# Maxima over all slots by VectorE's block transposes in place of TensorE's, in four of five groups

## The chip, the cores and the metric

The kernel runs on one core of a Trainium2 chip. A core has a matrix engine (TensorE, PE in the profile; its weight loads are listed apart as PEld), three engines for elementwise work (VectorE or DVE, ScalarE or ACT, GpSimd or POOL), a queue for transfers (SyncE or SP) and 16 DMA engines. Each engine works through its own queue in order, and engines wait for each other through semaphores. Matrix products are written to PSUM; the other operands lie in SBUF, on 128 partitions. The metric is the device time of one execution in microseconds, as a median over runs.

## The reference

Sixteen sequences of 100 tokens, 256 wide, go through cross attention to a context of 361 tokens (16 heads), and then through a soft mixture of 16 experts with 64 slots each. Everything is float32. What matters here is the second half, cut to its core:

```python
x = _layernorm(x, norm_g, norm_b)
se = _layernorm(slot_embeds, slot_g, slot_b) * scale
logits = jnp.einsum('bnd,esd->bnes', x, se)
dispatch = jax.nn.softmax(logits, axis=1)
combine = jax.nn.softmax(logits.reshape(x.shape[0], x.shape[1], -1), axis=-1)
slots = jnp.einsum('bnd,bnes->besd', x, dispatch)
gate = jax.nn.gelu(jnp.einsum('besd,edf->besf', slots, Wg) + bg, approximate=False)
up = jnp.einsum('besd,edf->besf', slots, Wu) + bu
eout = jnp.einsum('besf,efo->beso', gate * up, Wd) + bd
return jnp.einsum('bns,bso->bno', combine, eout)
```

`combine` is a softmax over all 1024 slots of a token. It needs, for each token, the largest logit over the slots. That maximum is what the change concerns.

## The kernel before

The 16 sequences are cut into groups of 2, 2, 4, 4 and 4 (`GROUPS`, line 51). A group goes through attention (`units`, line 862: for each sequence and each of four blocks of heads the scores, their maxima, the exponentials and the values), then through `dispatch_quarter` for each pair p of sequences and each quarter q of the 1024 slots, then through `combine_weights` for each pair, and at last through `experts` with `combine_quarter`. The experts of one group run beside the attention of the next.

The program is fixed when it is built. A planner in the kernel (`Clock`, line 64, and the loop from line 1361) keeps a modelled time for each engine; every piece of work is a generator that yields when it would be ready, how many PSUM banks it needs and, in some cases, the word "aside". At each step the planner issues the first piece in a list that is ready at the modelled time of PE (units and dispatches, then side work, then the experts). From the first expert on, a step marked "aside" is held until VectorE's modelled backlog is at most 2.5 us (`BACKLOG`, lines 1417 to 1421). Four PSUM banks, tiles tagged "mm", go round among all products except the attention scores. Of several `combine_weights` in the list only the first is looked at, so that pairs follow one another.

In `dispatch_quarter` (line 927) the logits of a pair lie with 128 slots on the partitions and (two slot blocks, two sequences, 100 tokens) along the row. They are copied to `lg_all` (line 963), and `top` (128 partitions by 2 by 100) takes the maximum over the blocks seen so far (lines 1064, 1065, 1068). After four quarters `top` holds on each partition the maximum over eight of the 1024 slots, and the maximum over the 128 partitions is still to come.

`combine_weights` (line 1073) does this with TensorE. Two transposes (line 1079) turn `top` into `top_t`, 100 tokens by 256, in PSUM; VectorE reduces each row (line 1081) to the negative maximum `c_mx`; VectorE multiplies the identity by it (line 1089), giving two diagonal matrices `dg`; a product of ones with `dg` (line 1093) puts the negative maximum of each token on all 128 partitions of `neg_top`; ScalarE copies it back into `top` (line 1100). A float32 product is two instructions in the profile, a transpose is one. Then GpSimd adds it to the logits of each quarter (line 1107), ScalarE takes the exponentials (line 1130), GpSimd sums them into `dg` (lines 1133, 1134, 1137), and a product with ones gives the sums over the slots (line 1119, `c_sums`), whose reciprocal `combine_quarter` uses. There are eight pairs in all, one in each of the first two groups and two in each of the others.

Three other places serve for comparison. `dispatch_quarter` transposes by VectorE within blocks of 32 from group 3 on (line 1012, `BY_DVE`). `key_work` does so for the context of sequences 4 and up (lines 598, 599). In attention, VectorE's reduction of line 790 (`mxp`) and the addition of line 801 (`q`) stand between products of PE (lines 785, 799, 810).

Of the kernel before, what the change touches and what calls it, by code (L numbers as in the profile page):

```python
# [33 lines left out]
F32 = mybir.dt.float32  # L34
AF = mybir.ActivationFunctionType
ALU = mybir.AluOpType
AX = mybir.AxisListType
# [3 lines left out]
B, N, D = 16, 100, 256  # L41
# [6 lines left out]
P = 128  # L48
# [81 lines left out]
def xattn_ffn_kernel(  # L130
# [27 lines left out]
    nc = tc.nc  # L158
    ctx.enter_context(tc.manual_schedule())
    ck = Clock(4)  # L160

    const = ctx.enter_context(tc.tile_pool(name="const", bufs=1))
    dram = ctx.enter_context(tc.tile_pool(name="dram", bufs=1, space=DRAM))
    two = ctx.enter_context(tc.tile_pool(name="two", bufs=2))
# [4 lines left out]
    def mm_tile(name):  # L169
        return ps_mm.tile([P, 512], F32, tag="mm", name=name)  # L170
# [52 lines left out]
    ident = const.tile([P, P], F32, name="ident")  # L223
# [105 lines left out]
    ones = const.tile([P, P], F32, name="ones")  # L329
# [439 lines left out]
    class Unit:  # L769
# [35 lines left out]
        def exponentials(self):  # L805

            for c in range(3):
                for r in range(4):
                    rows = slice(32 * r, 32 * r + 32)
                    nc.tensor.matmul(  # L810
                        self.at[: KC + 1, r, c * N : (c + 1) * N],
                        lhsT=self.k[rows, c * KC : c * KC + KC + 1],
                        rhs=self.q2[rows],
                        start=True,
                        stop=True,
                    )
            self.aT = two.tile([P, 4, 3 * N], F32, tag="aT", name="aT")
            nc.scalar.activation(self.aT[: KC + 1], self.at[: KC + 1, :, : 3 * N], AF.Exp)  # L818
            self.t = free_t[0] = ck.act("exp", 1080, ck.run("PE", 0.85, self.t))
            phase[0] = "exp"  # L820
            if self.cb == 3:
                live.discard(self.b)
# [104 lines left out]
    def dispatch_quarter(g, p, q):  # L927
# [142 lines left out]
        top[1] += 1  # L1070
        logits[g, p, q] = slot

    def combine_weights(g, p):

        yield (lambda: tops[g, p][2] if tops.get((g, p), (0, 0))[1] == NQ else NEVER), 1
        top, _, t = tops[g, p]
        tp = mm_tile("top_t")
        for i in range(2):
            nc.tensor.transpose(tp[:N, i * P : (i + 1) * P], top[:, i, :], ident)
        nm = two.tile([N, 2], F32, tag="c_mx", name="c_mx")  # L1080
        nc.vector.tensor_reduce(
            nm, tp[:N, : 2 * P].rearrange("n (i s) -> n i s", i=2), AX.X, ALU.max, negate=True
        )
        t = ck.psum_dve(256, ck.run("PE", 0.25, t, ck.bank()))
        ck.free(t)

        dg = const.tile([P, 2, N], F32, tag="dg", name="dg")
        for i in range(2):
            nc.vector.tensor_scalar_mul(dg[:N, i, :], ident[:N, :N], nm[:, i : i + 1])
            t = ck.run("DVE", 0.22)  # L1090
        yield t, 1
        ps = mm_tile("neg_top")
        nc.tensor.matmul(
            ps[:, : 2 * N],
            lhsT=ones[:N, :],
            rhs=dg[:N].rearrange("n i t -> n (i t)"),
            start=True,
            stop=True,
        )
        nc.scalar.copy(top.rearrange("p i n -> p (i n)"), ps[:, : 2 * N])  # L1100
        t = ck.copy(200, ck.pe(200, t, ck.bank()))
        ck.free(t)
        tq = [t]
        for q in range(NQ):
            yield tq[-1], 0
            w = lg_all[:, logits[g, p, q]].rearrange("p (c i) n -> p c i n", c=2)
            nc.gpsimd.tensor_tensor(w, w, top.unsqueeze(1).to_broadcast([P, 2, 2, N]), ALU.add)
            t = ck.run("POOL", 0.9, t)
            tq.append(t)
            if q:  # L1110
                yield tq[-2], 0
                tq[-2] = exponentials(g, p, q - 1, dg, tq[-2])
        yield tq[-1], 0
        t = exponentials(g, p, NQ - 1, dg, tq[-1])
        yield t, 1
        sm = const.tile([N, 2], F32, tag=f"c_sm{p}", name="c_sm", bufs=2)
        ps = mm_tile("c_sums")
        for i in range(2):
            nc.tensor.matmul(
                ps[:N, i : i + 1], lhsT=dg[:, i, :], rhs=ones[:, 0:1], start=True, stop=True  # L1120
            )
        nc.vector.reciprocal(sm, ps[:N, :2])
        t = ck.run("DVE", 0.2, ck.run("PE", 0.5, t, ck.bank()))
        ck.free(t)
        sums[g, p] = sm
# [235 lines left out]
    while streams["experts"]:  # L1361
        g = len(accs)
# [110 lines left out]
        if task.done:  # L1473
            fill[:] = [t for t in fill if t is not task]
            dispatches[:] = [t for t in dispatches if t is not task]
            for name, t in streams.items():
                if t is task:
                    streams[name] = None
                    if name == "units":
                        g = group - 1  # L1480
                        for p in range(GROUPS[g] // 2):
                            for q in range(NQ):
                                dispatches.append(Task(dispatch_quarter(g, p, q), ck, 2))
                            dispatches.append(Task(combine_weights(g, p), ck))
# [52 lines left out]
```

## Time and profile before

| what | value |
|---|---|
| median of 3 runs | 1176.27 us (1175.8 to 1177.32) |
| the profiled execution | 1176.62 us, its span 1174.70 us |
| granted TensorE clock, mean | 0.999 |
| DVE, ACT, POOL busy | 632.8 us, 542.9 us, 153.6 us |
| PEld busy | 899.3 us |
| first and last transpose of `top` (line 1079) | at 113.0 us and 1050.2 us |
| last `c_sums` (line 1119) | at 1072.2 us |

The span runs from the first to the last instruction; the 1.9 us by which the execution is longer lie outside it. In groups of instructions, `out<-in` are the program's names for tiles, and L1079 is line 1079 of the kernel. Busy time of PE is the union of its instructions' spans; since they overlap, the cost of one is better read from the distance between starts. In lists of waits the columns are the time in all, the number of waits and the longest. In listings of one line or tile, three durations in ns are the least, the median and the largest.

### The profile page before, as it was taken

Reading aid. Unit: us, or ns where it says so; the run is one execution under the profiler, and the core shown is the slowest. Engines: PE = TensorE matmul, PEld = TensorE weight load, DVE = VectorE, ACT = ScalarE, POOL = GpSimd, SP = SyncE. Lnnn points to the kernel's source line nnn. Section 1 sums busy time; section 2 is a strip of 40 time slices with the busy share of each in tenths; the row PEclk is TensorE's granted clock in tenths of the full one; section 3 lists DMA queues with packets and bytes.
Section 4 is the critical chain, followed back from the end, with each engine's and each line's share of the span. In section 5 each row is a group of like instructions: output and inputs, shape, how many; then the busy total and the mean of one; then the engine's idle time right before and its main releaser. Section 6 shows DMA issues by size and latency. Waiting matters only on the chain.

```text
span 1174.7 us, 24302 instructions
## 1 busy us (share of the span) xinstructions
PE 1159.4 (99%) x9825; PEld 899.3 (77%) x9825; DVE 632.8 (54%) x1561; ACT 542.9 (46%) x1112; POOL 153.6 (13%) x255
## 2 busy tenths in 40 slices
PE   8899999999999999999999999999999999999998
PEld 6587778778788777777777777787878878777876
DVE  5755545575644667644756655657533455432222
ACT  3557554655454765554435545446312336314110
POOL 3110301022000141400101000034000003002000
PEclk9999999999999999999999999999999999999999
DMA  4412656543467404232323213333344343345441
GB/s 134 137 38 99 233 174 203 163 148 114 139 213 233 115 20 86 78 113 95 83 80 108 95 38 113 113 126 112 113 155 145 113 149 127 112 132 161 138 131 55
DMA packets 138588, 144.85 MB, mean 123 GB/s; under 512 B 45050, under 2 KB 97228, under 8 KB 138476
## 3 DMA queue, kind: packets, MB, share of 16 engines
q1 hardware_dynamic: 137258, 141.50, 39.1%
q8 instruction: 78, 1.28, 0.5%
q0 software_dynamic: 496, 1.12, 0.3%
q10 hardware_dynamic: 722, 0.67, 0.2%
q14 instruction: 34, 0.28, 0.1%
HBM read 141.60 MB, written 1.66 MB: 122 GB/s over the span
## 4 chain that ended last, share of the span: by engine, by line
PE 97%; DVE 2%; ACT 1%; POOL 0%; issue 0%; DVEq 0%; POOLq 0%; ACTq 0%
PE gp L1291 20%; PE dn L1244 19%; PE up L1291 19%; PE sl L1032 5%; PE po L1162 5%; PE at L810 5%; PE at L785 4%; PE v_ps L673 4%; PE lg L942 4%; PE k_ps L613 3%; PE cx L833 3%; PE at L1344 1%; PE o_ps L726 1%; PE q_ps L538 1%; DVE mxp L790 1%; PE d_t L1020 1%
## 5 line engine op out<-in xcount | busy, mean ns | idle before, releaser
L1291 PE MATMUL gp<-ring,w_all 128*128 128x256 f32 (+1 forms) x1280 | 249.7, 341 | 1.8 <-ACT lg_all L963 1.3
L1291 PE MATMUL up<-ring,w_all 128*128 128x256 f32 (+1 forms) x1280 | 247.2, 339 | 0.0
L1307 DVE SCALAR_TENSOR_TENSOR hT<-up,parT,ge 128x256 f32<-128x256 f32 (+1 forms) x320 | 119.4, 423 | 224.6 <-PE up L1291 179.5
L1302 ACT ACTIVATE ge<-gp,parT 128x256 f32<-128x256 f32 (+1 forms) x320 | 116.9, 429 | 266.2 <-PE gp L1291 265.6
L1244 PE MATMUL dn<-w_all,hT 128*64 128x256 f32 x2048 | 232.5, 382 | 0.0
L1291 PEld LDWEIGHTS gp<-ring,w_all 128*128 128x128 f32 x1280 | 203.7, 191 | 30.1 <-issue 8.0
L1291 PEld LDWEIGHTS up<-ring,w_all 128*128 128x128 f32 x1280 | 205.0, 191 | 21.2 <-issue 0.8
L1244 PEld LDWEIGHTS dn<-w_all,hT 128*64 128x64 f32 x2048 | 142.4, 137 | 78.1 <-issue 8.9
L1253 DVE TENSOR_TENSOR ring<-dn,bd_bc 128x512 f32<-128x512 f32 x64 | 44.3, 692 | 144.0 <-PE dn L1244 143.9
L790 DVE TENSOR_REDUCE mxp<-at 100x4 f32<-100x1444 f32 x64 | 106.3, 1660 | 28.6 <-PE at L785 26.9
L818 ACT ACTIVATE aT<-at 121x1200 f32<-121x1200 f32 x64 | 74.9, 1170 | 49.3 <-PE at L810 45.0
L1302 ACT ACT_TABLE_LOAD x61 | 78.3, 1283 | 26.4 <-PE gp L1291 25.6
L1012 DVE STREAM_TRANSPOSE disp<-d_ex 32x128 f32<-32x128 f32 x256 | 77.3, 302 | 4.6
L717 POOL TENSOR_TENSOR cxs<-cxs,rs 128x100 f32<-128x100 f32 x63 | 24.9, 397 | 385.3 <-DVE rs L714 343.3
L1032 PE MATMUL sl<-disp,xn 100*128 100x256 f32 x256 | 63.0, 388 | 0.0
L997 POOL TENSOR_TENSOR d_ex<-d_ex,d_sm 128x400 f32<-128x400 f32 x28 | 23.7, 852 | 293.5 <-DVE d_sm L994 293.4
L1162 PE MATMUL po<-ring,lg_all 128*100 128x256 f32 x256 | 59.7, 382 | 0.1
L1047 ACT ACTIVATE ring<-sl,parT 128x256 f32<-128x256 f32 x64 | 32.6, 561 | 53.1 <-PE sl L1032 53.1
L810 PEld LDWEIGHTS at<-q,kT 32*121 32x121 f32 x1344 | 40.6, 180 | 19.8 <-issue 6.1
L818 ACT ACT_TABLE_LOAD x35 | 44.9, 1283 | 22.8 <-DVE q L801 12.5
L1032 PEld LDWEIGHTS sl<-disp,xn 100*128 100x128 f32 x256 | 46.6, 190 | 9.6 <-issue 2.8
L810 PE MATMUL at<-q,kT 32*121 32x100 f32 x1344 | 49.9, 277 | 3.6 <-DVE q L801 3.6
(152 smaller groups left out, 1273.0 us busy)
## 6 DMA issues: line engine op xcount, KB each, us to landing
w_all<-in_L_ffn_Wg_dram SPq DMA_DIRECT2D x80, 512.0 KB
w_all<-in_L_ffn_Wu_dram SPq DMA_DIRECT2D x80, 512.0 KB
w_all<-in_L_ffn_Wd_dram SPq DMA_DIRECT2D x80, 512.0 KB
bd_bc<-in_L_ffn_bd_dram SPq DMA_DIRECT2D x80, 64.0 KB
c_sb<-in_ctx_dram SPq DMA_DIRECT2D x96, 44.0 KB
acc<-in_x_dram SPq DMA_DIRECT2D x7, 200.0 KB
out_dram<-acc SPq DMA_DIRECT2D x7, 200.0 KB
ring<-n_L_ffn_slot_embeds_dram POOLq DMA_DIRECT2D x1, 1024.0 KB, 7.2
```

What stands on the lines that cost most here:

```text
L673: nc.tensor.matmul(ps[: KC + 1, :D], lhsT=cT[:, kd, c * KC : c * KC + KC + 1], rhs=w_sb["wv"][:, kd, :], start=kd == 0, stop=kd == KD - 1,)
L785: nc.tensor.matmul(self.at[:N, r, :S2], lhsT=self.q[rows], rhs=self.k[rows], start=True, stop=True)
L790: nc.vector.tensor_reduce(mxv[:, :, m : m + 1], self.at[:N, :, :S2], AX.X, ALU.max, negate=True)
L810: nc.tensor.matmul(self.at[: KC + 1, r, c * N : (c + 1) * N], lhsT=self.k[rows, c * KC : c * KC + KC + 1], rhs=self.q2[rows], start=True, ...
L818: nc.scalar.activation(self.aT[: KC + 1], self.at[: KC + 1, :, : 3 * N], AF.Exp)
L1012: nc.vector.transpose(dst[toks, :, :, a, :], src[32 * a : 32 * a + 32, :, :, toks])
L1032: nc.tensor.matmul(sl[:, kd * 256 : (kd + 1) * 256], lhsT=xns[g][:, b0 + i, kd * P : (kd + 1) * P], rhs=disp[:, i, :], start=True, stop=True,)
L1162: nc.tensor.matmul(pos[i][:N, :D], lhsT=lg_all[:, slot, 2 * c + i, :], rhs=eouts_of(g, q)[:, c, 2 * p + i, :], start=c == 0, stop=c == 1,)
L1244: nc.tensor.matmul(dn[S * x : S * x + S, i * D : (i + 1) * D], lhsT=hts[x][fc // FB][0].rearrange("p (f b s) -> p f b s", f=FB, s=S)[:, fc ...
L1291: nc.tensor.matmul(ps[:, f * T : (f + 1) * T], lhsT=w[:, kd, fc * P : (fc + 1) * P], rhs=slots_of(g, q)[:, j, kd].rearrange("p b s -> p (b ...
L1302: nc.scalar.activation(ge[:, cols], ps[:, cols], AF.Gelu, bias=col(8, e, fc))
L1307: nc.vector.scalar_tensor_tensor(out=hT[:, cols], in0=ps[:, cols], scalar=col(NPAR, e, fc), in1=ge[:, cols], op0=ALU.add, op1=ALU.mult,)
```

## The change

In groups 1 to 4 (seven of the eight pairs) the maximum over the 128 partitions is found by VectorE alone. The partitions are folded by two maxima, 128 to 64 and 64 to 32. The 32 rows that are left, padded from 100 to 128 tokens, are transposed within blocks of 32, so that the 32 partial maxima of a token lie in a row; they are reduced to the negative maximum, spread over 32 columns by a copy, and four more transposes of blocks, one for each quarter of the partitions, put the negative maximum of each token on all 128 partitions. GpSimd then adds from `m2` and not from `top`. Two tiles of 128 by 256 are set to zero by GpSimd once, at the first such pair. Group 0 keeps the old way. The steps are marked "aside"; their prices in the planner are 0.7, 1.0 and four times 0.35 us of VectorE.

```diff
+    maxs = []
+    MAX_DVE = 1
...
-        tp = mm_tile("top_t")
-        for i in range(2):
-            nc.tensor.transpose(tp[:N, i * P : (i + 1) * P], top[:, i, :], ident)
-        nm = two.tile([N, 2], F32, tag="c_mx", name="c_mx")
-        nc.vector.tensor_reduce(
-            nm, tp[:N, : 2 * P].rearrange("n (i s) -> n i s", i=2), AX.X, ALU.max, negate=True
-        )
-        t = ck.psum_dve(256, ck.run("PE", 0.25, t, ck.bank()))
-        ck.free(t)
-
         dg = const.tile([P, 2, N], F32, tag="dg", name="dg")
...
+        if g >= MAX_DVE and not maxs:
+            for i in range(2):
+                maxs.append(const.tile([P, 2, P], F32, name=f"maxs{i}"))
+                nc.gpsimd.memset(maxs[i], 0.0)
+        if g >= MAX_DVE:
+
+            m2, m1 = maxs[0], maxs[1]
+            yield t, 0, (0.0, 0.7, 0.0), "aside"
+            nc.vector.tensor_tensor(m2[:64, :, :N], top[:64], top[64:], ALU.max)
+            nc.vector.tensor_tensor(m1[:32, :, :N], m2[:32, :, :N], m2[32:64, :, :N], ALU.max)
+            t = ck.run("DVE", 0.7, t)
+            yield t, 0, (0.0, 1.0, 0.0), "aside"
+            flat1, flat2 = (m.rearrange("p i n -> p (i n)") for m in (m1, m2))
+            nc.vector.transpose(flat2[:32], flat1[:32])
+            nm = two.tile([32, 8], F32, tag="c_mx32", name="c_mx32")
+            nc.vector.tensor_reduce(
+                nm, flat2[:32].rearrange("p (j s) -> p j s", s=32), AX.X, ALU.max, negate=True
+            )
+            nc.vector.tensor_copy(
+                flat1[:32].rearrange("p (j s) -> p j s", s=32),
+                nm.unsqueeze(2).to_broadcast([32, 8, 32]),
+            )
+            t = ck.run("DVE", 1.0, t)
+
+            for a in range(4):
+                if a % 2 == 0:
+                    yield t, 0, (0.0, 0.7, 0.0), "aside"
+                nc.vector.transpose(flat2[32 * a : 32 * a + 32], flat1[:32])
+                t = ck.run("DVE", 0.35, t)
+            minus = m2[:, :, :N]
+        else:
...
+            minus = top
...
-            nc.gpsimd.tensor_tensor(w, w, top.unsqueeze(1).to_broadcast([P, 2, 2, N]), ALU.add)
+            nc.gpsimd.tensor_tensor(w, w, minus.unsqueeze(1).to_broadcast([P, 2, 2, N]), ALU.add)
```

Under `else` stand the old lines: the two transposes, the reduction, the two diagonal matrices, the product with ones and ScalarE's copy.

More of the change, by code (lines that the diff above doesn't have):

```diff
@@ L1088, in combine_weights @@
[L1088 to L1101, printed above, removed]
@@ L1102, in combine_weights @@
-        ck.free(t)
+        dg = const.tile([P, 2, N], F32, tag="dg", name="dg")
+        if g >= MAX_DVE and not maxs:
[27 more added lines that the diff above has]
+        else:
+            tp = mm_tile("top_t")
+            for i in range(2):
+                nc.tensor.transpose(tp[:N, i * P : (i + 1) * P], top[:, i, :], ident)
+            nm = two.tile([N, 2], F32, tag="c_mx", name="c_mx")
+            nc.vector.tensor_reduce(
+                nm, tp[:N, : 2 * P].rearrange("n (i s) -> n i s", i=2), AX.X, ALU.max, negate=True
+            )
+            t = ck.psum_dve(256, ck.run("PE", 0.25, t, ck.bank()))
+            ck.free(t)
+            for i in range(2):
+                nc.vector.tensor_scalar_mul(dg[:N, i, :], ident[:N, :N], nm[:, i : i + 1])
+                t = ck.run("DVE", 0.22)
+            yield t, 1
+            ps = mm_tile("neg_top")
+            nc.tensor.matmul(
+                ps[:, : 2 * N],
+                lhsT=ones[:N, :],
+                rhs=dg[:N].rearrange("n i t -> n (i t)"),
+                start=True,
+                stop=True,
+            )
+            nc.scalar.copy(top.rearrange("p i n -> p (i n)"), ps[:, : 2 * N])
+            t = ck.copy(200, ck.pe(200, t, ck.bank()))
+            ck.free(t)
+            minus = top
```

## The prediction

> **What bounds the kernel now.** I read the page first: busy time, then the chain of work that ended last.
>
> ```profile
> span 1174.7 us, 24302 instructions
> PE 1159.4 (99%) x9825; PEld 899.3 (77%) x9825; DVE 632.8 (54%) x1561; ACT 542.9 (46%) x1112; POOL 153.6 (13%) x255
> PE 97%; DVE 2%; ACT 1%; POOL 0%; issue 0%; DVEq 0%; POOLq 0%; ACTq 0%
> ```
>
> PE carries 97% of the chain, VectorE 2%. A busy PE is not yet a PE at its pace, so I then read what PE itself waited for, over the whole span (total us, times, longest).
>
> ```profile
> PE at L810 <- DVE q L801: 3.6, 9, 0.8
> ...
> PE gp L1291 <- ACT lg_all L963: 1.3, 1, 1.3
> PE c_sums L1119 <- POOL dg L1134: 1.0, 1, 1.0
> ...
> PE d_t L1020 <- ACT cxs L842: 0.5, 1, 0.5
> PE gp L1291 <- DVE hT L1307: 0.5, 1, 0.5
> ```
>
> The same list by stretches puts 3.0 of the 3.6 us at line 810 into the first 60 us, and only 2.2 us of waits of all kinds behind 250 us (1.0, 0.5, 0.2 and 0.5). The code is altered from the second pair on, whose transposes start at 251.9 us, so everything ahead of that should stay as it is. The table of busy time by stage (span of the stage, then PE, PEld, DVE, ACT, POOL) shows how much room the helpers have where the seven pairs lie.
>
> ```profile
> 240.00:415.00 175.00, 174.19 (x1885) 137.91 (x1884) 102.71 (x248) 100.57 (x202) 24.24 (x39) 1.00 0.52 161
> 415.00:500.00 85.00, 84.02 (x838) 63.08 (x839) 59.19 (x140) 48.32 (x110) 29.68 (x41) 1.00 0.25 64
> 758.00:830.00 72.00, 71.52 (x434) 56.44 (x434) 45.35 (x127) 33.79 (x68) 22.22 (x34) 1.00 0.38 126
> 975.00:1075.00 100.00, 100.00 (x594) 79.59 (x592) 44.61 (x119) 42.57 (x81) 18.93 (x25) 1.00 0.43 136
> ```
>
> PE is full in each; VectorE is at 59%, 70%, 63% and 45%. So the time is that of PE's queue, and an edit is worth what it takes out of that queue, less any hole that it opens.
>
> **What leaves PE.** Durations overlap, so I take distances between starts, from the order of time around the second pair (start us, us):
>
> ```profile
> 251.25 0.72 PE L833 MATMUL cx<-aT,vpad 120*32 120x100 f32 x24
> 251.91 0.42 PE L1079 MATMUL top_t<-ident,top 128*100 128x128 f32 x2
> 252.17 1.95 PE L1291 MATMUL up<-ring,w_all 128*128 128x128 f32 x16
> 253.95 0.25 PE L799 MATMUL at<-ident,mxp 100*128 100x100 f32 x1
> 254.09 0.58 PE L1093 MATMUL neg_top<-dg,ones 100*128 100x200 f32 x2
> 254.50 0.39 PE L1291 MATMUL gp<-ring,w_all 128*128 128x128 f32 x2
> ```
>
> The two transposes hold PE from 251.91 to 252.17, 0.26 us; the product with ones from 254.09 to 254.50, 0.41 us. The same reading for the seven pairs gives 0.26, 0.31, 0.26, 0.31, 0.22, 0.26 and 0.36 us for the transposes (1.98 in all) and 0.41, 0.43, 0.43, 0.54, 0.34, 0.34 and 0.44 us for the product (2.94): 4.92 us. From below, the steps inside these groups are 109 ns for a transpose and 169 ns for a half of the product, so 7 x (2 x 0.109 + 2 x 0.169) = 3.9 us is pure streaming, and the other 1.0 us is change-over between shapes, of which some may return at the new neighbours. From above, a down product that is followed by something else steps by 310 ns and not by 216, so 7 x 0.094 = 0.7 us more may go with the interruptions: 5.6 us. I take 4.9, the distances that were really there.
>
> **What leaves the others.** ScalarE loses seven copies of 0.33 us (2.3 us) and VectorE seven reductions of 0.42 and fourteen multiplications that take 0.45 us a pair: 0.87 us a pair. PSUM's four banks lose two uses a pair. None of it is on PE's path today: nothing in PE's list waits for `top_t`, `c_mx` or `neg_top`. I count 0.
>
> **What VectorE gains.** The trace has no operation on these very shapes, so I price by the nearest rows (least/median/largest ns):
>
> ```profile
> L1064 DVE TENSOR_TENSOR top<-top,lg_all x24: 347/356/368, 95.4 to 1046.6; 128x200 f32<-128x200 f32 x24
> L967 DVE TENSOR_REDUCE d_mx<-lg_all x28: 569/570/571, 210.4 to 1012.2; 128x4 f32<-128x400 f32 x28
> L1012 DVE STREAM_TRANSPOSE disp<-d_ex x256: 289/302/308, 565.8 to 1042.6; 32x128 f32<-32x128 f32 x128
> L598 DVE STREAM_TRANSPOSE cT<-c_sb x12: 855/910/915, 192.5 to 669.8; 128x704 f32<-128x704 f32 x12
> L418 DVE COPY ring<-pat x1: 400/400/400, 15.0 to 15.0; 128x256 f32<-128x256 f32 x1
> ```
>
> Two maxima over 200 elements: 2 x 0.36. Five transposes over 256: between 302 ns for 128 and 910 for 704 a straight line gives 0.44, so 2.2. One reduction of 256 elements: 0.42, as the one that goes. One copy with a repeated input: 0.40. Together 3.7 us a pair, net 2.9, over seven pairs 20 us on an engine that was busy for 633 of 1175. The bounds are wide: with 0.25 (line 801, 100 elements) for maxima, copy and each transpose (line 599, 64 elements) the work is 2.4 us a pair; with 0.91 for each transpose, 0.57 for the reduction and 0.69 for the copy (line 1253, 512 elements) it is 6.5. I take 3.7, since the rows on either side of 256 elements are close. The planner prices it at 3.1, so VectorE runs behind its plan by 0.6 us a pair (-0.7 to +3.4 by the bounds).
>
> What hides this is the plan: the work is in four pieces of about 0.8 to 1.3 us, each held while VectorE's backlog is over 2.5 us, and PE has products that do not need VectorE. Queued behind a piece are the attention's reduction (line 790) and addition (line 801), PSUM evacuations (lines 1307, 1253, 1044) and `d_mx`; behind those stand PE's lines 799 and 810 and the four banks. Without cover a pair costs PE up to 2.9 us, 20 us in all. Behind 250 us PE waited for VectorE 0.2 us at line 810 and 0.5 us at line 1291, so I cost it at 0, with 0 to 4.4 us (the lag of 0.6, seven times) as what may show.
>
> **New waits.** The first maximum waits for GpSimd's two zero fills: by the row of 128x112 in 0.19 us, about 0.44 each, 0.1 to 1.0. GpSimd is idle from 251.0 to 255.3, so they are done before VectorE comes to them; at worst 0.9 us of VectorE, once. Writing `m2` again waits for the adds of line 1107 of the pair ahead; the fourth add ends 12 to 17 us after its pair begins, and the pairs begin at least 43 us apart. The adds now wait for the last transpose in place of ScalarE's copy, which itself sat in ScalarE's queue (423.3 us for a product that ended at 420.6). So the sums come from some us earlier to some later; only `c_sums` and, far behind, `combine_quarter` wait for them, and the experts pass over a quarter whose sums are missing. `c_sums` already cost PE 0.98 us once, at 439.2 us, where a GpSimd addition took 2.08 us in place of 0.61.
>
> The Trainium skill, page SBUF — State Buffer, section "SBUF: two separate sides", says that VectorE and GpSimd lock a pair of SBUF ports against each other for whole instructions, where VectorE reads two SBUF inputs or uses both ports. By it the two maxima and the copy, 1.1 us a pair, could each hold GpSimd up, 7.8 us in all, and if all of that reached `c_sums` the time would be 1179.5 us. The trace has long additions (2.08 and 1.78 us), but VectorE was then mostly in line 790's reduction from PSUM, and a pair's own additions start after its maxima; I leave the sum as it is.
>
> **Sum.** 1176.6 - 4.9 + 0 = 1171.7 us, against the profiled execution's own time (span 1174.7, and 1.9 outside). That execution is 0.35 us above the median of the runs.
>
> **Rivals.**
> *The gain is given back (1174 to 1178, about 1176).* A new order of all that follows 250 us opens new holes. The lag of 0.6 us a pair, if it all shows, is 4.4 us: 1176.1. For it: `c_sums` and line 810 do wait at times. Against it: 2.2 us of holes in 925 us says that the plan fills nearly everything.
> The Trainium skill, page Perfetto Trace Analysis, section "Identifying the Most-Contended Engine", warns that matmul occupancy is no measure, and points to weight-load time, here 77%; by that PE would have room and the removal might bring nothing, 1176.6. The starts speak against it: 16 instructions of 128 columns from 252.17 to 253.95 us are 111 ns each, the pace at which that line runs wherever nothing interrupts it.
> *Slower: VectorE becomes late in attention (about 1185).* Place: the stretches at 251 to 273, 415 to 500 and 758 to 830 us. Each of the 28 pieces lands in front of a line 801 that PE is about to need and moves it by half its 0.93 us: 13 us of holes, 1176.6 - 4.9 + 13 = 1184.7. It decides from 7.3 us of holes on (4.9 + 2.4), 1.0 us a pair. For it: VectorE is 70% busy at 415 to 500. Against it: the pieces are short and kept back.
> *More than forecast (about 1169).* Besides 4.9 the holes of 0.98 and 0.48 us beside pairs at 439 and 803 us close, and 0.7 of change-overs goes: 7.1 us, 1169.5.
>
> **Chances.** Forecast (a gain of 3.0 to 6) 0.58; given back 0.20; slower 0.10; more 0.12. A difference of 0.2%, 2.35 us, is about what a measurement of this kernel can tell. So faster is 0.58 + 0.12 = 0.70, same 0.20, slower 0.10. The range goes from the last rival's time, 1169.0, to most of the first's, 1177.0; above it lie the slower case and a little of the first, below it a little of the last.
>
> **What would show it.** Right: PE has 28 instructions fewer (14 transposes, 14 halves of products), PE's waits behind 250 us stay at 1 to 4 us, VectorE is busy for about 653 us, ScalarE for about 540, and 1174.7 less the new span is the PE time that went. Wrong: new lines of some us in PE's waits at lines 799, 810 or 1119, named for VectorE or GpSimd; transposes of 32x256 far above 0.44 us; or a longer PE total although instructions went, which would mean more change-overs in the new order.

## The result and the profile after

The changed kernel takes 1172.79 us (median of 7 runs, 1171.94 to 1174.15) against 1176.57 us of the kernel before in 7 runs: the ratio is 0.9964, with a 95% interval of 0.9954 to 0.9974. That is 3.8 us less by the medians, where 4.9 were forecast. The profiled execution took 1172.79 us, with a span of 1171.0.

The page of the changed kernel, its span, busy times and chain:

```profile
span 1171.0 us, 24299 instructions
PE 1155.7 (99%) x9797; PEld 895.9 (77%) x9797; DVE 651.2 (56%) x1602; ACT 563.9 (48%) x1124; POOL 152.0 (13%) x257
...
PE 95%; ACT 2%; DVE 2%; issue 0%; ACTq 0%; POOL 0%; DVEq 0%; POOLq 0%
```

PE has 28 instructions fewer (9825 to 9797) and 3.7 us less busy time, and the span is 3.7 us shorter. VectorE has 18.4 us more. ScalarE has 21 us more, which nothing in the change asks for; that is taken up below. What PE waited for in the changed kernel (total us, times, longest), without the rows that belong to the first 100 us:

```profile
PE xn_t L752 <- DVE d_sm L994: 1.0, 1, 1.0
...
PE sl L1032 <- ACT disp L1025: 0.7, 3, 0.3
PE po L1197 <- DVE ring L1288: 0.2, 1, 0.2
PE sl L1032 <- DVE acc L1208: 0.2, 1, 0.2
```

These are 2.1 us behind 250 us, as the 2.2 us before, but they are other waits: the one at `c_sums` is gone, and a new one stands at `xn_t` (410 us). The planner has a new order, and its holes lie elsewhere. VectorE's new instructions, each with least, median and largest ns:

```profile
L1084 POOL MEMSET maxs<- x2: 309/310/310, 251.7 to 251.9; 128x256 f32 x2
L1089 DVE TENSOR_TENSOR maxs<-top x7: 360/361/363, 253.9 to 1048.2; 64x200 f32<-64x200 f32 x7
L1090 DVE TENSOR_TENSOR maxs<-maxs x7: 353/355/897, 254.3 to 1048.6; 32x200 f32<-32x200 f32 x7
L1094 DVE STREAM_TRANSPOSE maxs<-maxs x7: 419/423/423, 258.3 to 1051.5; 32x256 f32<-32x256 f32 x7
L1096 DVE TENSOR_REDUCE c_mx<-maxs x7: 406/406/407, 258.8 to 1052.0; 32x8 f32<-32x256 f32 x7
L1099 DVE COPY maxs<-c_mx x7: 280/280/282, 259.2 to 1052.4; 32x256 f32<-32x256 f32 x7
L1108 DVE STREAM_TRANSPOSE maxs<-maxs x28: 375/435/439, 262.5 to 1059.4; 32x256 f32<-32x256 f32 x28
```

A pair costs 0.36 + 0.36 + 0.42 + 0.41 + 0.28 + 4 x 0.435 = 3.57 us of VectorE.

### The profile page after: what moved, and what is told of

Its sections match the earlier page's. It is cut to its first block, busy times and chain, and to the rows that moved or that the text cites. A ratio compares the mean times of both kernels' runs of the same rounds, so it can differ in the third digit from the quotient of the medians.

```text
span 1171.0 us, 24299 instructions
## 1 busy us (share of the span) xinstructions
PE 1155.7 (99%) x9797; PEld 895.9 (77%) x9797; DVE 651.2 (56%) x1602; ACT 563.9 (48%) x1124; POOL 152.0 (13%) x257
## 4 chain that ended last, share of the span: by engine, by line
PE 95%; ACT 2%; DVE 2%; issue 0%; ACTq 0%; POOL 0%; DVEq 0%; POOLq 0%
PE gp L1326 20%; PE dn L1279 20%; PE up L1326 19%; PE sl L1032 5%; PE po L1197 4%; PE at L810 4%; PE at L785 4%; PE lg L942 3%; PE v_ps L673 3%; PE cx L833 3%; PE k_ps L613 3%; PE at L1379 1%; PE o_ps L726 1%; DVE mxp L790 1%; PE q_ps L538 1%; ACT d_ex L972 1%
## 5 line engine op out<-in xcount | busy, mean ns | idle before, releaser
L842 ACT COPY cxs<-cx 128x100 f32<-128x100 f32 x64 | 15.7, 245 | 85.3 <-PE cx L833 84.1
```

## The experiments

The theory to test, "PE queue", is that of the prediction: the gain is the TensorE time that went, and VectorE's work is free. Its rivals: the gain is that of the planner's new order; or VectorE's work costs holes, and the gain is larger than it seems less a cost. Eleven kernels ran, all compared with the kernel before. The expectations stand as they were written ahead of the runs.

### TensorE's work put back in the new order

```diff
             yield t, 0, (0.0, 0.7, 0.0), "aside"
+            for i in range(2):
+                nc.tensor.transpose(at_all[:N, 3, 384:], top[:, i, :], ident)
             nc.vector.tensor_tensor(m2[:64, :, :N], top[:64], top[64:], ALU.max)
...
             t = ck.run("DVE", 1.0, t)
+            for i in range(2):
+                nc.tensor.matmul(at_all[:, 3, 384 : 384 + N], lhsT=ones[:N, :], rhs=ones[:N, :N], start=True, stop=True)
```

> The changed kernel in its new order, with TensorE's work of the seven pairs put back (two transposes, and the product with ones as two products of 100 columns, into an unread corner of PSUM); the planner isn't told, and nobody reads the results. Theory 'PE queue' (the gain is the TensorE time that went): 4.9 us come back, 1177.7 us, ratio to before 1.000 to 1.002. Rival 'order' (the gain is the planner's new order, with its four uses of a bank and its waits): stays near 1173, ratio 0.996 to 0.998. Rival 'other engines' (ScalarE's copies and the wait for them): stays near 1173 too.

Measured: 1188.64 us, ratio 1.0098 (1.0084 to 1.0112), 15.9 us above the change. That is too much for either theory. What PE waited for in it:

```profile
PE at L1107 <- ACT aT L818: 4.2, 2, 2.1
PE at L1090 <- DVE mxp L790: 3.9, 4, 1.2
```

Lines 1090 and 1107 are the two products that were put back. They wait for the readers of the attention's tile, into whose corner they write, and PE's queue stands behind them. So this run tells nothing of the theories, and the next kernel puts the same work where it waits for nobody.

### TensorE's work put back in a bank of its own

```diff
             m2, m1 = maxs[0], maxs[1]
+            ps = mm_tile("top_b")
+            for i in range(2):
+                nc.tensor.transpose(ps[:N, i * P : (i + 1) * P], top[:, i, :], ident)
+            nc.tensor.matmul(ps[:, 256 : 256 + 2 * N], lhsT=ones[:N, :],
+                rhs=top[:N].rearrange("n i t -> n (i t)"), start=True, stop=True)
+            ck.free(ck.bank())
             yield t, 0, (0.0, 0.7, 0.0), "aside"
```

> The changed kernel in its new order, with TensorE's work of the seven pairs put back once more, now into a bank of the four that go round, at the step where the planner has one free, and not into the corner of the attention's tile, for which TensorE had to wait: two transposes and a product of 200 columns, results read by nobody, the planner not told. Theory 'PE queue': 4.9 us come back, 1177 to 1179, ratio 0.9995 to 1.0020. Rival 'order': stays near 1173, ratio 0.9955 to 0.9975. Waits for a bank would show as new rows in TensorE's waits and are to be taken off.

Measured: 1176.15 us, ratio 0.9992 (0.9984 to 1.0001). Against the change's 0.9964 that is 0.28% more, 3.3 us. PE's waits behind 250 us are the change's own, within 0.1 us a row. By distances between starts the work now holds PE for 1.79 + 2.48 = 4.27 us, since transposes and product stand together and have one change-over less. All other instructions of PE and of ScalarE run in the order that they have in the change. The same down products start later than in the change by 1.2 us behind the first three pairs (0.79 after -0.39), where the work holds 1.8 us, and by 3.7 at the end (3.28 after -0.39): the later four pairs cost 2.5 us, all that their work holds. So TensorE's time comes back nearly whole. "PE queue" holds, "order" falls as the source of the gain, and so do ScalarE's copies and VectorE's diagonal matrices, which are away in this kernel too: by the medians 0.5 us of the 3.8 is left for them and the rest.

### The new work in the old order, and VectorE's work alone

In the first kernel each instruction that stays keeps its place, and VectorE's chain stands where the old instructions stood. The second is the kernel before, with the chain added and its result unused.

```diff
 # new_work_old_order, where g is not 0: prices and yields of before
-        two transposes, tensor_reduce, two tensor_scalar_mul
+        tensor_tensor, tensor_tensor, transpose, tensor_reduce, tensor_copy
         yield t, 1
-        matmul, scalar.copy
+        four transposes
 # vector_work_added, where g is not 0: ahead of the product with ones
         yield t, 1
+        tensor_tensor, tensor_tensor, transpose, tensor_reduce, tensor_copy, four transposes
```

> The change's work in the old order: in the seven pairs VectorE's chain stands where TensorE's instructions, the diagonal matrices and ScalarE's copy stood, and the planner is priced as before, so that every other instruction keeps its place. Theory 'PE queue': 4.9 us less, plus 0 to 1 us for a chain that is placed unplanned: 1172 to 1173, ratio 0.996 to 0.997. Rival 'order': no gain, 1176 to 1177.

> The kernel before in its old order, with VectorE's whole chain of the change (nine instructions, about 3.5 us a pair in one piece) added in the seven pairs ahead of the product with ones; the planner isn't told, and nobody reads the results. Theory 'PE queue, VectorE free': 1176 to 1178 us, ratio 0.999 to 1.002. Rival 'VectorE costs holes' (the change gains more than it seems and loses some of it to VectorE): 1180 to 1200, up to 3.5 us a pair, 24 us in all.

Measured: 1180.4 us, ratio 1.0025 (1.0016 to 1.0034), for the new work in the old order, and 1186.48 us, ratio 1.0077 (1.0064 to 1.0090), for VectorE's work alone. Both contradict the theory in its second half: VectorE's work is not free by itself. The change's work in the old order makes the kernel slower.

Since the order is the same, the start of one and the same down product can be compared from trace to trace. The table gives by how much it is later than in the kernel before, in us; the change itself can be compared only where its order has come together with the old one again. Pairs start at 252, 417, 463, 759, 802, 976 and 1050 us.

| down product that starts, before, at | VectorE's work alone | new work, old order | groups 3 and 4 only | the change |
|---|---|---|---|---|
| 108.6 | 0.5 | 0.6 | 0.4 | 0.7 |
| 276.3 | 2.8 | 2.1 | 0.4 | |
| 498.7 | 9.2 | 5.4 | 0.5 | |
| 730.4 | 9.2 | 5.4 | 0.5 | |
| 789.7 | 9.2 | 4.4 | -0.4 | |
| 894.6 | 10.9 | 4.9 | -1.4 | -2.2 |
| 997.8 | 10.9 | 4.4 | -2.3 | -3.1 |
| 1096.9 | 10.9 | 3.5 | -3.0 | -3.7 |

The first row lies ahead of any edit: up to 0.7 us is what executions differ by at their start. VectorE's work alone costs 8.7 us over the first three pairs; of the four later pairs only the one at 802 us costs something, 1.6. Not all of the 8.7 us is waiting for VectorE. From 478.0 to 481.4 us, behind PE's longest wait of that kernel (2.3 us at line 799), the granted TensorE clock was 0.51, and half of that stretch, 1.7 us, is an estimate of what it cost. The eight products behind that wait took 3.25 us there and 1.91 in the kernel before; in order of time, with VectorE's work alone and then before:

```profile
477.64 3.25 PE L1313 MATMUL gp<-ring,w_all 128*128 128x256 f32 x8
```

```profile
470.09 1.91 PE L1291 MATMUL gp<-ring,w_all 128*128 128x256 f32 x8
```

Another 0.4 us is a wait for a weight transfer between the pairs. That leaves about 6.6 us, 2.2 a pair. The new work in the old order loses 4.8 us net at the first three, where 2.1 us of TensorE went; later it loses 0.5 at the pair at 802 us and gains at the other three. What PE waited for in it:

```profile
PE at L799 <- DVE mxp L790: 3.0, 2, 1.9
PE c_sums L1148 <- POOL dg L1163: 2.4, 2, 1.4
...
PE x_t L519 <- DVE z L504: 1.1, 3, 0.6
```

The longest of them in order of time, VectorE and PE of the same kernel:

```profile
471.50 1.72 DVE L1117 STREAM_TRANSPOSE maxs<-maxs 32x256 f32<-32x256 f32 x4
473.25 1.66 DVE L790 TENSOR_REDUCE mxp<-at 100x4 f32<-100x1444 f32 x1
```

```profile
471.11 1.92 PE L1320 MATMUL up<-ring,w_all 128*128 128x256 f32 x8
474.97 0.30 PE L799 MATMUL at<-ident,mxp 100*128 100x100 f32 x1 [1.95 <-DVE mxp L790]
```

Four transposes run on VectorE from 471.50 to 473.22, and only then the attention's reduction starts; PE has run out of the products that the planner put in between and waits 1.95 us at line 799. A piece of VectorE's work that is not in the plan goes straight to PE here, because attention goes to and fro between the two engines.

### The planner's part: steps not held

```diff
-            yield t, 0, (0.0, 0.7, 0.0), "aside"
+            yield t, 0
```

and the same for the other three steps.

> The changed kernel with the word 'aside' taken off its four steps: the planner knows VectorE's prices, but no longer holds a step while VectorE's modelled backlog is over 2.5 us. Theory 'the holding makes VectorE free': holes at lines 799 and 810 behind 250 us, 2 to 8 us, 1175 to 1181. Rival 'knowing the prices is enough': 1172 to 1174, as the change.

Measured: 1175.63 us, ratio 0.9981 (0.9972 to 0.9990): 0.17% above the change, 2.0 us. Not all of it is the edit's. In the profiled execution the granted TensorE clock was 0.83 from 40 to 50 us, far ahead of the first edited step, and 1.00 there in the change (this kernel's stretch: its span, then PE, PEld, DVE, ACT, POOL, granted clock, DMA):

```profile
40.00:50.00 10.00, 7.94 (x86) 5.10 (x88) 5.99 (x16) 6.20 (x12) 3.48 (x4) 0.83 0.65 190
```

The first down product of the table (108.6) is 1.9 us later than in the kernel before, where no other kernel here is later by more than 0.8. Five of the 11 executions show a mean granted clock of 0.999 or 1.000, and their median is 1174.26 us, ratio 0.9975; the other six, at 0.998, lie at 1175.63 or more. In the trace this kernel gains 2.7 us from the first down product to the end (1.9 later to 0.8 earlier), where the change gains 4.5. So holding the steps is worth 1.3 to 1.7 us. Most comes from a plan that knows the prices (0.9975 to 0.9981, against 1.0025 for the same work unplanned), though the orders of these two kernels differ in all that follows. The new hole in this kernel:

```profile
PE at L785 <- ACT aT L818: 1.1, 1, 1.1
```

It stands at 428 us, in attention, and not at line 799 or 810 as I had expected: ScalarE's exponentials wait behind those of a dispatch, which wait for VectorE.

### Which pairs bring the gain

```diff
 # half_the_pairs
-    MAX_DVE = 1
+    MAX_DVE = 3
 # groups_1_and_2_only
-        if g >= MAX_DVE:
+        if g in (1, 2):
 # all_groups
-    MAX_DVE = 1
+    MAX_DVE = 0
```

> The changed kernel with the new way from group 3 on only: four pairs in place of seven. Theory 'PE queue': the four pairs held 2.75 us of TensorE by distances between starts (1.14 for the transposes, 1.66 for the product, of 4.92 for seven): 1173.8 us, ratio 0.9976. Rival 'order': no relation to the number of pairs, anywhere from 1170 to 1180.

> The changed kernel with the new way in groups 1 and 2 alone (three pairs, at 252, 417 and 463 us), the old way in groups 0, 3 and 4. Theory 'PE queue' alone: the three pairs held 2.1 us of TensorE, ratio 0.9982. Theory 'VectorE is free only where there is room': in these stretches half or all of it is lost in holes, 0 to 1.1 us gained, ratio 0.9990 to 1.0000.

> The changed kernel with the new way in the first group too, eight pairs in place of seven. Theory 'PE queue': the first pair held TensorE for 0.26 + 0.34 = 0.60 us, so 0.6 us below the changed kernel, ratio to before about 0.9958; at that place (113 us) VectorE was busy for about half of the time. Rival 'VectorE costs holes': the same or slower than the changed kernel.

Measured: 1173.44 us, ratio 0.9966 (0.9954 to 0.9979), for groups 3 and 4, as "PE queue" has it within the interval; 1176.46 us, ratio 0.9994 (0.9985 to 1.0003), for groups 1 and 2; 1173.98 us, ratio 0.9972 (0.9960 to 0.9984), for all groups. The four pairs of groups 3 and 4 bring nearly all: by the table 3.4 us (from 0.4 to -3.0), where 2.8 us of TensorE went; about 0.5 more is a hole at 803 us that closed (PE's wait of 0.48 us at line 1291 in the kernel before). The three pairs of groups 1 and 2 bring 0.06%, not to be told from nothing, and 0.8 us by the starts in their trace (0.66 at 108.6 us, -0.11 behind 894.6), where 2.1 us of TensorE went: the second theory's case. The eighth pair, in group 0, adds nothing that shows; 0.9958 was forecast for it by "PE queue", and lies outside the interval.

### How much room VectorE has

The chain four times, planned like the change; and another piece of work moved from TensorE to VectorE.

```diff
 # chain_four_times: ahead of the chain, into a third tile, same yields and prices
+            for _ in range(3):
+                two maxima, transpose, reduction, copy, four transposes
 # dispatch_by_vector_from_group_2
-    BY_DVE = 3
+    BY_DVE = 2
```

> The changed kernel with VectorE's chain done four times in each of the seven pairs (three times into a tile that nobody reads), with the same yields and prices, so that the planner knows of it: about 3.5 x 21 = 73 us more of VectorE. Theory 'PE queue, VectorE free where it is planned': within 2 us of the changed kernel, 1172 to 1175. Rival 'VectorE costs holes': 1177 to 1195, a hole or more at each of the 84 pieces added.

> The changed kernel with the transposes of the dispatch weights given to VectorE from group 2 on and not from group 3: eight quarters less of four TensorE transposes at about 0.58 us a quarter, 4.7 us of TensorE, and 128 VectorE transposes of 0.30 us more, 39 us, between 400 and 500 us, where VectorE was 66% busy. Theory 'PE queue' without regard to VectorE: 1168 us, ratio 0.9925. Theory 'VectorE is free only up to its load in that stage': VectorE reaches 39 + 56 us of some 85 to 100, and the time is 1172 to 1185.

Measured: 1183.71 us, ratio 1.0060 (1.0047 to 1.0072), for four chains, 11 us above the change with 72.6 us more of VectorE: 0.15 us of time for each us of VectorE, planned. That is the rival's range: planned work isn't free once there is so much of it. Behind 250 us PE's longest waits in this kernel are for VectorE (3.7 us at line 613, 2.6 at line 1032). And 1206.94 us, ratio 1.0254 (1.0240 to 1.0268), with the dispatch by VectorE from group 2 on: both expectations of the time were too low, 30 us lost where 4.7 us of TensorE went. The stretch from 390 to 490 us of that kernel, and then of the kernel before (span, then PE, PEld, DVE, ACT, POOL, granted clock, DMA):

```profile
390.00:490.00 100.00, 74.01 (x663) 50.95 (x659) 83.46 (x219) 38.42 (x104) 20.13 (x29) 0.81 0.19 42
```

```profile
390.00:490.00 100.00, 98.24 (x986) 74.55 (x985) 70.28 (x163) 62.31 (x147) 32.77 (x44) 1.00 0.26 66
```

At 83% VectorE is now the busiest engine, and PE is idle for 26 us. PE's named waits from 390 to 500 us are 9.7 us for ScalarE's exponentials (line 785) and 12.8 us for VectorE's reductions and additions in attention (lines 799 and 810).

### Less of VectorE for the same result

The last four transposes give the same 32 by 256 block to each quarter of the partitions. Here the first is kept, and GpSimd copies its result to the other three.

```diff
-                nc.vector.transpose(flat2[32 * a : 32 * a + 32], flat1[:32])
+            nc.vector.transpose(flat2[:32], flat1[:32])
+            for a in range(1, 4):
+                nc.gpsimd.tensor_copy(flat2[32 * a : 32 * a + 32], flat2[:32])
```

> The changed kernel with three of its last four transposes replaced by three copies of the first one's result by GpSimd to the other quarters of the partitions; the planner is priced 0.45 for VectorE and 0.6 for each copy. VectorE has 1.3 us less a pair, 9 us in all; GpSimd, 13% busy, some 2 us more a pair. Theory 'VectorE is free only where there is room': up to 1 us of what groups 1 and 2 lose comes back, 1172 to 1173, ratio 0.9955 to 0.9965. Rival: the sums come later by GpSimd's copies and TensorE waits at line 1154 for them, 1173 to 1177.

Measured: 1172.1 us, ratio 0.9956 (0.9943 to 0.9968), the lowest of all; its interval overlaps the change's (0.9954 to 0.9974), so that it is ahead of the kernel before for certain and ahead of the change only by its median. The copies:

```profile
L1109 POOL COPY maxs<-maxs x21: 387/393/417, 262.5 to 1055.5; 32x256 f32<-32x256 f32 x21
```

No wait at `c_sums` appears, and VectorE is busy for 636.7 us against 651.2. The order is a new one here as well, so the difference of 0.7 us isn't shown to be VectorE's.

## Why the prediction was right, and where it was not

**PE's queue sets the time, and 4.9 us leave it: right.** The instructions that went are the 28 that were counted. Put back in the new order they hold PE for 4.3 us and cost 3.3 to 3.7. The trace of the change gains 4.5 us behind the first edit (from 0.7 later to 3.7 earlier); by the medians it is 3.8.

**VectorE's price: right in size.** Forecast 3.7 us a pair, measured 3.57; the transposes at 0.42 and 0.435 stand where the straight line put them (0.44), the copy took 0.28 and not 0.40, the zero fills 0.31 and not 0.44. VectorE's total came out as forecast (651 us for 653); ScalarE's did not (564 for 540, see the last section).

**"I cost it at 0": the term that was mis-sized, and its reason was half wrong.** On their own, the three pairs of groups 1 and 2 gave 0.8 us of their 2.1; 1.3 us were lost. Part of this was in the rival "given back", for which 0.20 was allowed; it happens in groups 1 and 2 alone, and the other pairs made up for some of it by closing a hole of 0.5 us, as the rival "more than forecast" had it. So the total lies near the forecast in part by luck: a loss and a gain that were both left out of the sum offset each other. I had argued from PE's full columns that the plan would cover VectorE's work. That work is covered, and not wholly, because its steps are priced and, for the last 1.3 to 1.7 us, held. The uncovered price that the prediction gave, "up to 2.9 us" a pair, was an upper end: VectorE's work alone cost about 2.2 at the first three pairs, when the lower clock and the wait for a transfer are taken off, in stretches where VectorE is 59% to 70% busy and stands between PE's products of attention. At the other end, three of the four late pairs cost nothing even unplanned: there PE works on experts, and no product of attention waits for VectorE.

**The slower rival had the mechanism but not the case.** Work of VectorE lands in front of the reduction of line 790 and PE waits at line 799: this is what happened in the old order (ratio 1.0025), and not in the change, whose plan keeps the pieces out of the way.

**New waits: right in what they cost, for other reasons.** The zero fills ran at 251.7 us, ahead of the first maximum at 253.9. `c_sums` has no wait left in the change; in the old order it had 2.4 us.

**The ports that VectorE and GpSimd share: seldom, as taken.** One of the fourteen maxima was held up for long, in the changed kernel, VectorE and GpSimd:

```profile
423.90 0.90 DVE L1090 TENSOR_TENSOR maxs<-maxs 32x200 f32<-32x200 f32 x1
```

```profile
423.61 0.96 POOL L997 TENSOR_TENSOR d_ex<-d_ex,d_sm 128x400 f32<-128x400 f32 x1 [11.57 <-DVE d_sm L994]
```

It took 0.90 us, 0.54 more than its median, and ended 0.23 us behind GpSimd's multiplication, which had begun first. That is in keeping with the exclusive lock that the Trainium skill describes (SBUF — State Buffer, "SBUF: two separate sides"). The price of it in the whole kernel is 0.6 us of VectorE (0.54, and 0.09 for another at 722 us). The 7.8 us that the prediction gave as an end were for the other direction, GpSimd held up by VectorE. Of that the trace shows 0.11 us in this multiplication (0.96 for a usual 0.85), which began beside the first maximum, and about as much in the operation at 722 us; no copy of the change ran beside an operation of GpSimd.

**Weight loads at 77% are no headroom here.** By weight-load time, which the Trainium skill names, beside the share of the peak arithmetic, as the measure of TensorE's headroom (Perfetto Trace Analysis, "Identifying the Most-Contended Engine"), PE would have had room to take the work back for nothing; it cost 3.3 to 3.7 us. The distance between starts was the measure that held.

What stays open: where the 1.3 us of groups 1 and 2 go. The waits that the trace names behind 250 us add up to about the same as before (2.1 us in the change and 2.5 with groups 1 and 2 alone, against 2.2). The transposes of `d_t` take 0.95 us more than before by distances between starts, but that is no further loss: the wait of 1.05 us at `xn_t` stands behind the last of one group of them, at 410 us, and is in this sum already. With groups 1 and 2 alone, other steps became longer without a named wait, those of `up` by 0.5 us in all and those of `sl` by 0.4. And the new order has room on PE there, since the work that was put back cost 1.2 us of the 1.8 that it held. Whether the longer steps are change-overs or short waits was not settled.

## What to carry to other kernels

On a kernel whose matrix engine is full, an operation moved off it is worth up to the distance between starts that it held, which can be read ahead of time: here 4.9 us, of which 3.8 by the medians came out. Work added to an engine that is half idle on average cost least where no chain goes to and fro between the two engines; where one does, a plan that knows its price and keeps it in short pieces saved most of the cost but not all; look at each stage by itself, and try the moved work in the old order once, to see what the plan has to hide. Where a piece of it can go to a third engine that consumes the result anyway, as GpSimd's copies here, that is worth a try; here it was level with the change or a little ahead.

## What the runs showed of the hardware

The granted TensorE clock fell behind long waits of PE, but not behind all. In the dispatch experiment the slices of 10 us from 430 to 440, 440 to 450 and 480 to 490 us show a granted clock of 0.50, and the stretch of 100 us a mean of 0.81, with PE idle for a quarter of it. With VectorE's work alone it was 0.51 from 478.0 to 481.4 us, behind a wait of 2.3 us that ended at 477.5. With the chain four times it was 0.83 from 980 to 990 us, behind one of 2.6 us that ended at 983.0, and in the first kernel with TensorE's work put back 0.83 from 470 to 480 and from 730 to 740 us, behind waits of 2.1 us. But in the kernel with four chains it was 1.00 from 398 to 402 us, behind one of 3.7 us that ended at 398.8. The new work in the old order kept 1.00 behind its wait of 1.95 us, and with the steps not held the slice from 40 to 50 us shows 0.83 with no wait of PE over 0.9 us in it. So these traces don't give the rule. PE's busy time over the kernel of the dispatch experiment rose to 1164.4 us although it had 32 instructions fewer than the change (9765 to 9797). A hole on PE can therefore cost more than itself; how much of the 30 us this was, no run separates.

ScalarE's 21 us more in the change are table loads, of 1.283 us each: 140 in place of 122, 23 us. The planner's new order alternates more often between exponentials and the activations of the experts: there are 9 more at the activations (line 1337) and 8 more at attention's exponentials (line 818). With groups 3 and 4 only there are 124, at the same time within the measurement, but there three pairs also keep TensorE's work; what the loads cost the kernel, if anything, is not shown.
